# One-operation match in the expert routes, two pauses beside attention, and a layernorm applied by ScalarE alone

## The chip, the cores and the metric

The kernel runs on one core of a Trainium2 chip. The metric is the device time of one execution in microseconds (us). A core has TensorE (PE, with its weight load PEld), VectorE (DVE), ScalarE (ACT), GpSimd (POOL) and SyncE (SP), each with its own instruction queue; they run side by side and wait for each other by semaphores.

## The reference

The input is `x` of 8 batches, each 512 tokens of 128 numbers, in 32-bit floats. Six layers of different kinds are added to it one after the other:

```python
x = x + 0.5 * _L0_ffn_ref(_layernorm(x, axis=-1), L0_ffn_w_gate, L0_ffn_w_up, L0_ffn_w_down)
x = x + _L0_attn_ref(_layernorm(x, axis=-1), L0_attn_Wq, L0_attn_Wk, L0_attn_Wv, L0_attn_Wo, L0_attn_bo)
x = x + 0.5 * _L0_ffn_ref(_layernorm(x, axis=-1), L0_ffn_w_gate, L0_ffn_w_up, L0_ffn_w_down)
x = x + 0.5 * _L1_ffn_ref(_layernorm(x, axis=-1), L1_ffn_Wg, L1_ffn_W1, L1_ffn_W2, L1_ffn_W3)
x = x + _L1_attn_ref(_layernorm(x, axis=-1), L1_attn_w_qkv, L1_attn_w_out, L1_attn_b_out, L1_attn_gamma, L1_attn_beta)
x = x + 0.5 * _L1_ffn_ref(_layernorm(x, axis=-1), L1_ffn_Wg, L1_ffn_W1, L1_ffn_W2, L1_ffn_W3)
```

`_L0_ffn_ref` is a gated feed-forward whose inputs and weights are quantized to 4-bit floats in blocks of 16. `_L0_attn_ref` is softmax attention with 16 heads of 64 numbers. `_L1_ffn_ref` is a mixture of 8 experts with hidden size 256: every token goes to its two best experts, and their results are added with the softmax of the two scores as weights:

```python
top_v, top_i = jax.lax.top_k(gate_out, K)
probs = jax.nn.softmax(top_v, axis=-1)
...
    w_e = jnp.sum(probs * (top_i == e), axis=-1)
```

`_L1_attn_ref` is "efficient attention" of 6 layers: keys are normalized over the features and queries over the tokens, and `context = k^T v` (128x128) replaces the table of all pairs. The layernorm that the kernel calls `y` stands in front of its first layer: the residual stream inside `_L1_attn_ref` begins with a normalized `x`.

## The kernel before

A batch is held as `xs[b]`, 128 partitions by 4 chunks (`NC`) by 128. The first stage computes the feed-forward of all batches, interleaved with attention. Attention goes over 64 pairs of heads (`g`). The order of TensorE's and SP's work is written out by hand there: a list of steps (scores `pS`, projections `pq`, `pk`, `pv`, transposes `pT`, products `po`, output `py`) is run through once for each `g`. One kind of step, "ffn", calls `beside()`: it takes one step from a queue of other plans, that is, it issues that plan's instructions up to and with its next TensorE operation. `plan.pause()` puts an empty step into a plan, so that its next TensorE operation comes one "ffn" step later. The feed-forwards after attention of batches 0 to 6 and the first route stand in that queue, one behind the other; the feed-forward of batch 6 is the last.

After attention everything is ordered by a planner, `Plan.order`, before the kernel is built: each operation has an engine and an estimated time, and among those ready, the engine takes the one with the lowest key, the offset of its stage in the table `LATER` minus the longest path of estimates behind it. What comes out is one fixed order for each engine. Pauses are skipped there. The stages are: feed-forward of batch 7; phase 0 of the experts for batches 0 to 3 (A) and 4 to 7 (B); efficient attention over pairs of batches (k = 0, 2, 4, 6); phase 1 of the experts for A and B.

A stage of experts consists of a route, the gathering of tokens by expert, the expert products, and a combine. The route (`class Route`) scores the tokens (`gate`), picks the two best experts (`choose`, VectorE), counts tokens before each token with two products (`ranks`, L1035 and L1036), turns the counts into places in a table of slots (`bases`, `places`), and inverts this table: for each of 40 columns (`NR`) and 128 rows, which token sits there. The inversion goes over 8 parts (`tokens_part`), each for 4 chunks of tokens:

- `match` (L1125, VectorE): is the token's slot column equal to the column number? 128x160 into `in_slot`.
- `code` (L1140, GpSimd): `in_slot` times the number of the token, `code_no`, 128x160.
- `match_rows` (L1133, VectorE): is the token's row equal to the row number? 128x512 into `at_row`.
- `sums` (L1148, TensorE): four products of `at_row` and `in_slot` into one bank.
- `add` (L1156, L1158, VectorE): the bank into `acc`.

After the last part, `tables` (L1173 to L1179, VectorE) makes `tokens`, which the gathers read (L1215, an indirect DMA issued by GpSimd), and `targets` makes `places`, for the scatters (L1331). The buffers `in_slot` and `at_row` alternate between two, so that a match waits for the sums two parts before; in the first route, beside attention, there is one buffer of each. The route is computed four times: in the first route, B of phase 0, A and B of phase 1.

The expert stage has `g` (L1272 to L1277) and products at L1267 and L1315. The combine gathers the results token by token (L1384, GpSimd) and adds them to `x` (L1392, VectorE).

A layernorm (`class Norm`) takes its sums on VectorE (L390), and the reciprocal root in a chain of small GpSimd operations (`newton`, L369 to L374). It is applied by `on_vector` (L407, VectorE, one tensor_scalar for each chunk) or `on_scalar` (L415, ScalarE, one activation for each chunk). In `linear`, `begin` makes `y` from `x` with three chunks on VectorE and one on ScalarE; each of the 6 layers then applies its own layernorm with two chunks on each, and GpSimd adds a bias of 128x512 to `y` (L1466).

In the tail of attention L457, L468 and L469 are the quantizing of a feed-forward's hidden values on VectorE, L582 and L600 its last products; L708 is the row maximum `nmax`, L771 the division `oT`, which waits for `r`, the reciprocal row sums that go through a DMA (`wide`), L804 the output products.

## Time and profile before

| what | us |
|---|---|
| median of 3 timed runs | 2004.69 (2001.33 to 2011.76) |
| the profiled execution's own time | 1894.55 |
| its span | 1892.8 |
| TensorE, granted clock | 0.945 of full |
| GpSimd, busy | 962.0 |

The profile is of one execution. Its page splits the span into 40 equal slices (47.3 us each) and gives the busy tenths of every engine and the granted clock in tenths:

```profile
PE   3799999999999999999998998889659998798980
DVE  5475766775685776676657657557879998667543
ACT  2566666665665675666763654434457776353540
POOL 2345453443453453443443537676664444375786
PEclk8899999999999999999998999889979999698995
```

Slices 3 to 24 are the attention stage, 25 to 28 phase 0 of the experts, 29 to 35 efficient attention, and the rest phase 1. A digit 9 means 90% or more. The chain that ended last, by engine and by line:

```profile
PE 50%; DVE 23%; ACT 10%; POOL 9%; issue 4%; DMA 2%; SPq 0%; POOLq 0%; ACTq 0%; DVEq 0%
```

The share of an engine in the chain says how much of the span was spent waiting for it along one path; it is an average over stages with different limits.

### The profile page before, as it was taken

The numbers are of one execution on the slowest core, as the hardware profiler recorded it, in microseconds if no ns is written. First come the engines' busy times: TensorE is split into PE (matmuls) and PEld (weight loads), VectorE is DVE, ScalarE is ACT, GpSimd is POOL, SyncE is SP. The second block draws the span as 40 slices with busy tenths as digits, with TensorE's granted clock in tenths as the row PEclk, the third lists the DMA queues.
The fourth block names the chain that finished last, engine by engine and source line by source line (L and its number), as shares of the span: only waits on it lengthen the run. The fifth ranks groups of instructions, "written<-read, shape, count | busy, mean of one in ns | idle before, by whom it ended". The sixth has DMA issues, their size and how long they took to land.

```text
span 1892.8 us, 32338 instructions
## 1 busy us (share of the span) xinstructions
PE 1676.1 (89%) x10249; PEld 1132.1 (60%) x10249; DVE 1281.7 (68%) x3266; ACT 1073.6 (57%) x2842; POOL 962.0 (51%) x1643
## 2 busy tenths in 40 slices
PE   3799999999999999999998998889659998798980
PEld 2455656656556556556665566666548877676650
DVE  5475766775685776676657657557879998667543
ACT  2566666665665675666763654434457776353540
POOL 2345453443453453443443537676664444375786
PEclk8899999999999999999998999889979999698995
DMA  5477668567765776775683772215100000022314
GB/s 168 103 171 178 137 153 187 140 150 171 160 158 146 165 171 140 164 176 134 174 185 93 181 171 80 58 43 122 48 15 1 2 1 1 23 68 54 75 53 127
DMA packets 439253, 215.10 MB, mean 114 GB/s; under 512 B 349648, under 2 KB 392848, under 8 KB 439088
## 3 DMA queue, kind: packets, MB, share of 16 engines
q1 hardware_dynamic: 428608, 192.95, 42.7%
q0 software_dynamic: 9536, 19.55, 4.5%
q8 instruction: 86, 1.41, 0.3%
q14 instruction: 79, 0.65, 0.1%
q10 hardware_dynamic: 944, 0.54, 0.1%
HBM read 28.53 MB, written 100.53 MB: 68 GB/s over the span
## 4 chain that ended last, share of the span: by engine, by line
PE 50%; DVE 23%; ACT 10%; POOL 9%; issue 4%; DMA 2%; SPq 0%; POOLq 0%; ACTq 0%; DVEq 0%
PE po L763 9%; PE pS L699 9%; PE bank L1267 4%; ACT pe L711 4%; PE pT L749 3%; DVE nmax L708 3%; PE bank L600 2%; PE pv L685 2%; PE bank L541 2%; PE bank L1315 2%; PE pk L677 2%; PE bank L1148 2%; PE pq L671 2%; PE bank L424 2%; POOL work L1384 2%
## 5 line engine op out<-in xcount | busy, mean ns | idle before, releaser
L711 ACT ACTIVATE pe<-pS,nmax 128x512 f32<-128x512 f32 x512 | 348.4, 688 | 167.6 <-DVE nmax L708 135.8
L708 DVE TENSOR_REDUCE nmax<-pS 128x2 f32<-128x1024 f32 x256 | 310.6, 1214 | 75.7 <-PE pS L699 75.3
L720 POOL COPY pe_h<-pe 128x1024 uint16<-128x1024 uint16 x256 | 271.6, 1087 | 148.1 <-ACT pe L711 72.8
L699 PE MATMUL pS<-kT,qT 64*128 64x512 f32 x1024 | 291.9, 647 | 0.2
L763 PE MATMUL po<-aT,v 128*64 128x256 f32 x2048 | 239.2, 384 | 1.6 <-ACT kT L679 0.8
L787 POOL COPY wide<-rsum 128x512 uint16<-128x512 uint16 x128 | 76.4, 626 | 294.1 <-DVE rsum L783 294.1
L763 PEld LDWEIGHTS po<-aT,v 128*64 128x64 f32 x2048 | 142.9, 138 | 117.7 <-ACT pe L711 22.7
L1267 PE MATMUL bank<-wall,xgT 128*128 x320 | 156.8, 630 | 9.2 <-ACT xgT L1255 7.3
L749 PE MATMUL pT<-ident,pe 128*128 128x128 f32 x1024 | 137.3, 275 | 4.7 <-ACT pe L711 4.6
L749 PEld LDWEIGHTS pT<-ident,pe 128*128 128x128 f32 x1024 | 116.8, 141 | 23.1 <-ACT pe L711 17.8
L752 ACT COPY aT<-pT 128x512 f32<-128x512 f32 x192 | 107.5, 599 | 24.7 <-PE pT L749 23.0
L1272 ACT ACTIVATE g<-bank 128x256 f32<-128x256 f32 x160 | 61.0, 384 | 94.0 <-PE bank L1267 78.7
L699 PEld LDWEIGHTS pS<-kT,qT 64*128 64x128 f32 x1024 | 77.7, 186 | 57.8 <-issue 43.1
L1276 DVE SCALAR_TENSOR_TENSOR g<-g,bank 128x256 f32<-128x256 f32 x160 | 66.8, 417 | 64.9 <-ACT g L1272 64.5
L562 DVE SCALAR_TENSOR_TENSOR h<-h,bank 128x176 f32<-128x176 f32 x120 | 39.4, 329 | 100.7 <-ACT h L559 100.7
L541 PEld LDWEIGHTS bank<-wgu,xqT 128*128 128x128 f32 x480 | 76.2, 194 | 47.9 <-issue 20.4
L711 ACT ACTIVATION_READ_ACCUMULATOR pe<-pS,nmax 128x1 f32 x512 | 103.7, 202 | 0.0
L1267 PEld LDWEIGHTS bank<-wall,xgT 128*128 128x128 f32 x320 | 58.8, 199 | 73.5 <-issue 33.0
L541 PE MATMUL bank<-wgu,xqT 128*128 128x176 f32 x480 | 96.3, 327 | 6.3 <-ACT xqT L537 4.3
L771 DVE TENSOR_TENSOR oT<-po,r 128x256 f32<-128x256 f32 x128 | 52.0, 419 | 66.5 <-DMA r<-wide_d 34.5
L424 PE MATMUL bank<-ident,work 128*128 128x128 f32 x436 | 69.8, 289 | 28.1 <-DVE work L407 25.6
L685 PEld LDWEIGHTS pv<-wv_sb,hT 128*128 128x128 f32 x512 | 66.3, 193 | 43.5 <-ACT aT L752 21.7
(400 smaller groups left out, 3668.6 us busy)
## 6 DMA issues: line engine op xcount, KB each, us to landing
pe_d<-pe_h SPq DMA_DIRECT2D x256, 256.0 KB, 2.4
wide_d<-wide SPq DMA_DIRECT2D x64, 256.0 KB, 2.1
aT<-pe_d SPq DMA_TRANSPOSE x256, 3.8
xg<-work SPq DMA_DIRECT2D x12, 256.0 KB, 2.5
yg<-yo SPq DMA_DIRECT2D x10, 256.0 KB, 3.4
yt<-yo SPq DMA_DIRECT2D x10, 256.0 KB, 2.4
x<-in_x SPq DMA_DIRECT2D x8, 256.0 KB, 4.4
yk<-yg SPq DMA_DIRECT2D x8, 256.0 KB, 4.2
```

The lines of the kernel that those rows point to most:

```text
L424: nc.tensor.transpose(ps[:, c, :], src[:, c, :], ident)
L541: nc.tensor.matmul(ps[:, j * FH : (j + 1) * FH], m["xqT"][:, c * P : (c + 1) * P], wgu[:, j, cols], start=True, stop=True,)
L685: nc.tensor.matmul(ps[:, c, :], hT[:, c * P : (c + 1) * P], wv_sb[:, cols(g)], start=True, stop=True,)
L699: nc.tensor.matmul(ps[:, j, :], qTs[g][rows, c * P : (c + 1) * P], kTs[g][rows, :], start=True, stop=True,)
L708: nc.vector.tensor_reduce(nmax, ps, AX.X, ALU.max, negate=True)
L711: nc.scalar.activation(pe[:, j, :], ps[:, j, :], AF.Exp, bias=nmax[:, j : j + 1], accum_out=sums[g][:, 2 * c + j : 2 * c + j + 1],)
L720: nc.gpsimd.tensor_copy(split, pe[:, j, :].bitcast(U16).rearrange("p (n h) -> p h n", h=2))
L749: nc.tensor.transpose(ps[:, k, :], pe[:, j, k * P : (k + 1) * P], ident)
L752: nc.scalar.copy(dst, ps)
L763: nc.tensor.matmul(po[rows, :], vs[g][:, k, rows], aT[:, :, j, k, :], start=(k == 0), stop=(k == NC - 1),)
L787: nc.gpsimd.tensor_copy(split[:, h, :].rearrange("p (n d) -> p n d", d=DH), src[:, h, :, None].to_broadcast([P, NC * 2, DH]),)
L1267: nc.tensor.matmul(ps, xT[:, s, :], wall[:, bass.ds(at[s], 2 * HID)], start=True, stop=True)
```

## The change

The change has four parts. In each part of a route `match` becomes four tensor_scalar operations on VectorE (128x40 each, one for each chunk), which compare and multiply with the token's number in one operation; `code` on GpSimd is gone. Three pauses are put between `choose` and `ranks`, and two in front of the eight parts; they act in the route beside attention. `begin` applies the layernorm `y` with four activations on ScalarE. The planner's table `LATER` has other offsets, and the estimate of a match is 4 x 130 ns.

```diff
 LATER = {
-    ("combine", 0, 0): -5000,
-    ("combine", 0, 1): 6600,
-    ("combine", 1, 0): -15100,
-    ("combine", 1, 1): 199700,
-    ("experts", 0, 0): 3300,
-    ("experts", 1, 0): 90500,
-    ("experts", 1, 1): -37300,
-    ("ffn",): 11300,
-    ("linear", 0): 10800,
-    ("linear", 2): 6800,
-    ("linear", 4): -300,
-    ("linear", 6): 4600,
-    ("route", 0, 0): -10000,
-    ("route", 0, 1): -27200,
-    ("route", 1, 0): -6400,
-    ("route", 1, 1): 76900,
+    ("combine", 0, 1): 10915,
+    ("combine", 1, 0): 27994,
+    ("combine", 1, 1): -28254,
+    ("experts", 0, 0): 3252,
+    ("experts", 1, 0): 90518,
+    ("experts", 1, 1): -127932,
+    ("ffn",): -188793,
+    ("linear", 0): 10802,
+    ("linear", 2): 6768,
+    ("linear", 6): 4568,
+    ("route", 1, 0): -3116,
+    ("route", 1, 1): 76948,
 }
...
             ch = plan.add("DVE", 12 * 290 + 600, choose, taken)
+            for _ in range(3):
+                plan.pause()
             rk = plan.add("PE", product(n * E, 2), ranks, [ch], bank=True)
...
                 def match(_):
-                    bc = [P, NC, NR]
-                    ins = r["in", k] = mem(f"in_slot{k % 2}", bc)
-                    nc.vector.tensor_tensor(
-                        ins, r["slot"][:, j, cs, None].to_broadcast(bc),
-                        numbers[:, None, :NR].to_broadcast(bc), ALU.is_equal,
-                    )
+                    ins = r["in", k] = mem(f"in_slot{k % 2}", [P, NC, NR])
+                    for i in range(NC):
+                        c = q * NC + i
+                        nc.vector.tensor_scalar(
+                            ins[:, i, :], numbers[:, :NR], r["slot"][:, j, c : c + 1],
+                            code_no[:, j * NN + c : j * NN + c + 1], ALU.is_equal, ALU.mult,
+                        )
...
-                def code(_):
-                    bc = [P, NC, NR]
-                    nc.gpsimd.tensor_tensor(
-                        r["in", k], r["in", k],
-                        code_no[:, j * NN + q * NC : j * NN + (q + 1) * NC, None].to_broadcast(bc),
-                        ALU.mult,
-                    )
-
...
-                w = plan.add("DVE", dve(NC * NR), match, [pl, *users[-2:-1]])
-                w = plan.add("POOL", pool(NC * NR), code, [w])
+                w = plan.add("DVE", 4 * 130, match, [pl, *users[-2:-1]])
...
+            for _ in range(2):
+                plan.pause()
             for k in range(2 * MG):
                 tokens_part(k)
...
             def part(i, b):
-                op = plan.add("DVE", 3 * 343, lambda _: ln.on_vector(ys[b], xs[b], i, [0, 1, 2]), [ln.op])
-                op2 = plan.add("ACT", 390, lambda _: ln.on_scalar(ys[b], xs[b], i, [3]), [ln.op])
-                return [op, op2]
+                return plan.add(
+                    "ACT", 4 * 290 + 100, lambda _: ln.on_scalar(ys[b], xs[b], i, range(NC)), [ln.op]
+                )
```

Over four routes of eight parts this takes away 32 VectorE operations of 128x160 and 32 of GpSimd, and adds 128 VectorE operations of 128x40; in `begin` 24 operations go from VectorE to ScalarE.

## The prediction

> **What bounds the kernel now.** I read the table of busy shares first, then stretches of the span one by one, because the kernel is a row of stages with different limits; then, in each stage that the change touches, the waits of the engine that sets its pace. First the busy share, then the windows (stretch, length, busy PE, PEld, DVE, ACT, POOL with counts, TensorE clock, DMA share, GB/s):
>
> ```profile
> PE 1676.1 (89%) x10249; PEld 1132.1 (60%) x10249; DVE 1281.7 (68%) x3266; ACT 1073.6 (57%) x2842; POOL 962.0 (51%) x1643
> 1000.00:1050.00 50.00, 41.07 (x259) 27.42 (x258) 37.29 (x107) 18.35 (x46) 19.64 (x32) 0.86 0.40 102
> 1200.00:1300.00 100.00, 89.33 (x414) 62.56 (x414) 57.34 (x186) 37.19 (x82) 70.20 (x95) 0.85 0.28 73
> 1395.00:1472.16 77.16, 69.14 (x491) 58.23 (x492) 72.20 (x238) 53.66 (x183) 41.12 (x121) 0.98 0.01 1
> 1472.16:1515.68 43.52, 41.45 (x303) 35.14 (x303) 40.22 (x133) 32.82 (x121) 20.59 (x60) 1.00 0.00 1
> 1740.00:1893.00 153.00, 99.56 (x554) 69.32 (x552) 66.80 (x186) 54.92 (x120) 115.74 (x149) 0.84 0.35 86
> ```
>
> Attention (to 1138.7) is TensorE's: full, except in 1000 to 1050, where the first route runs beside it and TensorE loses 9 us. Phase 0 of the mixture of experts (1139 to 1339) is TensorE's with holes. In the linear-attention stage TensorE and VectorE are both above 92% of a 43.5 us layer. After 1740 GpSimd decides; see the last part of the change.
>
> **The route beside attention.** TensorE's timeline (start, length, line, operation, idle before and who ended it), then the tile `in_slot` with its waits:
>
> ```profile
> 1020.86 1.93 PE L1148 MATMUL bank<-in_slot,at_row 128*128 128x40 f32 x8 [8.27 <-POOL in_slot L1140]
> 1022.72 2.08 PE L699 MATMUL pS<-kT,qT 64*128 64x512 f32 x4
> 1024.72 5.57 PE L763 MATMUL po<-aT,v 128*64 128x256 f32 x32
> L1125 DVE TENSOR_TENSOR in_slot<-slot,numbers x8: 314/316/772, 1019.6 to 1052.2; 128x160 f32<-128x160 f32 x8
> L1140 POOL TENSOR_TENSOR in_slot<-in_slot,code_no x8: 766/768/886, 1020.0 to 1052.7; 128x160 f32<-128x160 f32 x8
>   POOL in_slot L1140: 20.3, 8
> ```
>
> TensorE stands 8.27 us until the first code operation ends. What follows is slow too: these three groups take 1.93, 2.08 and 5.57, where the same forms take 1.08, 1.13 and 3.67 from 1030 on, so 3.7 more. Two later parts make it wait 0.66 each. Together 8.3 + 3.7 + 1.3 = 13.3 us. The Trainium skill (TensorE: Matmul & The Clock Gate, Part 1) says that the array falls to half clock after an idle stretch of about 3.4 us and needs about as long of work to leave it. This bears on the new stall below.
>
> In the changed program's order the pauses put the ranks products a step later, with 11.7 us of TensorE work (four pS, po, pq, pk, pv, pT by their rows) between them and the first sums. VectorE needs 11.5 to 12.4 us from ranks to the first match. I take a wait of 1 us, too short to cool the clock: gain 12.3. If the cover fails, the wait is at most the old one.
>
> The price of a part: 4 tensor_scalar of 128x40 in place of one 128x160. No row has this form. A lone 128x40 tensor_scalar takes 0.18, and small VectorE operations start 0.11 to 0.22 after each other; four are 0.45 at the least, 0.8 at the most, I take 0.6 for four, against the 0.25 between starts of L1125 and L1133 now: +0.35. The skill speaks against the split: VectorE: DVE Perf Modes (The TRN2 errata) has a fixed 58 cycles per instruction at 0.96 GHz from SBUF, paid per tile, hence (58+160)/0.96 = 227 ns against 4 x (58+40)/0.96 = 408, +0.18. Over 32 parts that is +5.8 by the rule and +11.2 by my rows; I take the rows, since 316 was measured where the rule has 227. It matters only in the routes after attention, where a part's chain sets the pace. Against it stand 32 GpSimd operations of 0.77 to 0.83 (25.6 us) and two handovers a part. A second rule speaks against it: Advanced Engine Details and Errata (VectorE Performance Modes) says that two-port VectorE operations and GpSimd block each other. The trace agrees:
>
> ```profile
> 1659.43 0.83 DVE L1173 TENSOR_SCALAR tok_A<-acc_A 128x40 f32<-128x40 f32 x1
> 1658.95 1.27 POOL L1466 TENSOR_TENSOR y<-y,bout_sb 128x512 f32<-128x512 f32 x1 [0.23 <-DVE acc_A L1158]
> ```
>
> The 0.18 us form lasts until GpSimd's bias ends (1660.22). GpSimd computes in about 27% of 1000 to 1050 without the code operations; some 0.2 us a part, hidden by attention's TensorE work once sums stand one to a step. By the rule all 8 parts could wait up to 1 us; even that is under the roughly 3 us between parts.
>
> **The end of attention gives part back.** The five pauses push the last feed-forward's (ffn 6) products back five steps. Now the L600 product stands between the last pS and the last pT and covers the softmax:
>
> ```profile
> 1120.72 0.76 DVE L771 TENSOR_TENSOR oT<-po,r 128x256 f32<-128x256 f32 x2 [3.35 <-DMA r<-wide_d]
> 1121.39 1.21 DVE L708 TENSOR_REDUCE nmax<-pS 128x2 f32<-128x1024 f32 x1
> 1121.25 2.94 PE L600 MATMUL bank<-wdn,hqT 128*128 128x128 f32 x24
> ```
>
> In the changed order the last nmax stands behind L457, L468 and L469 of ffn 6 (0.81 each between starts = 2.4), which stand behind or between the two oT, and L468 waits 1.0 for ScalarE's h_mg: nmax 3.4 later, exp, pT, rsum and the r round trip with it (7.1 from rsum to oT). On the old times TensorE would stand from 1121.3 to about 1126.8 and still have L600 to do, which then fills the wait for r: the end moves by 5.5 or so. By the rule above such a stop also cools the clock (up to +3); by the row alone it doesn't. I take +6; ends 0 (the wait for r falls away) and +9. **Attention: -12.3 + 6 = -6.3**, ends -12 and 0. The early gathers (1058 to 1070, used at 1139) move some us and have room.
>
> **Phase 0, route B** (1222 to 1245). A part's chain is match, handover, 0.83 code, handover, sums; codes start 1.7 apart, with expert gathers queued between them on GpSimd. Without them a part is 0.83 + 0.15 - 0.35 = 0.6 shorter; six parts in a row give 4. TensorE does expert work meanwhile, but waits for those gathers (0.8 to 0.9, three times) and for g (2.98). **-4**, ends -10 and +5, since the planner's changed keys permute the order here most: route (0,1) goes from -27200 to 0, so later, and ffn 7 from 11300 to -188793, so ahead of the experts; TensorE's instructions are the same 7211 either way, so only waits can change, and the row of nearest size is the three waits above, 2.5 together.
>
> **Combine and linear attention.** GpSimd's gathers for combine B (1.25 each) stand in front of the first layer's rstd:
>
> ```profile
> 1386.57 2.14 PE L424 MATMUL bank<-ident,work 128*128 128x128 f32 x8 [24.70 <-DVE work L407]
> 1403.98 6.45 DVE L407 TENSOR_SCALAR y<-x,y_m,y_g 128x128 f32<-128x128 f32 x6
> 1404.18 6.16 POOL L1466 TENSOR_TENSOR y<-y,bout_sb 128x512 f32<-128x512 f32 x5
> ```
>
> The layernorm's six y operations (1.6 by their usual start distance) take 6.45 because they block with five biases: 4.8 lost. With the change ScalarE does all 24 of VectorE's: +24 x 0.41 = 9.9 us for an engine 71% busy, -24 x 0.26 = -6.2 for the one at 92%. A pair starts 0.9 later (4 activations, 1.66, in a row). In the new GpSimd order the first layer's rstd stands some three gathers earlier (-3.7) while the last combine ends 2 to 3 later. -4.8 - 3.7 + 0.9 + 2.5 = **-5**; ends -15 (more of the 24.7 closes) and +5.
>
> **Phase 1.** Route A (1637 to 1661): TensorE waits 8.29 and 2.73; codes sit between biases. Parts run in pairs of 2.6 us of VectorE: **-3** (-6 to +2). Route B (1715 to 1740): match pairs already wait for sums, and expert operations between them fill the time: **0** (-3 to +3).
>
> **The end.** From here GpSimd never idles:
>
> ```profile
> 1740.41 0.94 POOL L1215 DMA_INDIRECT y<-xg,tokens_B  x1 [3.17 <-DVE tokens_B L1179]
> 1883.98 0.94 POOL L1384 DMA_INDIRECT work<-yt,rows_A  x1 [0.30 <-issue]
> ```
>
> 39 gathers, 39 scatters, 32 combine gathers, the same number after: the end shifts with tokens_B, and everything above counts only through it. SP's and DMA's counts do not change.
>
> **Sum.** -6.3 - 4 - 5 - 3 = -18.3. The profiled execution took 1894.55 (span 1892.8), so about 1876 for it. The timed median, 2004.69, lies 110 above; nothing in the trace explains that, so I carry the difference in us: **1986**.
>
> **Rivals.** (a) *The gain is returned*: 0.25. The tail of attention goes cold (+9 instead of +6), route B of phase 0 gives nothing since TensorE is 89% busy there, and combine and route A give 1 each: -3.3 - 0 - 1 - 1 = about -5, 1999. For it: three of four gains lie under other work. Against it: the 13.4 us are TensorE's own. (b) *Slower*: the re-planned linear stage. The chain has the layers:
>
> ```profile
> 1472.16 1.47 DVE work L407 x2
> 1515.68 1.53 DVE work L407 x2
> ```
>
> 3.3 us of 43.5 are free on VectorE. Biases block L407 by about 1 us each, three times a layer now. If the new order lets all eight meet one, a layer takes 48.5, six layers +30: -18 + 30 = +12, 2017. It decides from 3 us a layer. Against it: the order stays near cyclic and counts are the same. 0.15. (c) *More*: the 24.7 us wait closes by ten more and route stalls vanish: -32, 1973. 0.15. (d) *It does nothing where it counts*: tokens_B does not move, as experts alone set it; contained in (a). Forecast: 0.45.
>
> A difference under 0.5% (10 us) can't be told from none. The forecast's own range is 1977 to 1996. Faster: 0.9 x 0.45 + 0.15 = 0.56; slower: 0.15 x 0.8 + some of (a)'s bad end (0.10) = 0.22; same 0.22. The range 1965 to 2018 leaves out the ends of (b) and (c).
>
> **What would show it.** The wait at L1148 near 1020 under 2 us, and no slow po behind it; a wait of about 5 before the last pT; attention ending near 1132; y in ScalarE rows; layer starts still 43.5 apart; tokens_B about 18 earlier. It is wrong if layers grow by over 1 us or tokens_B stays at 1740.

## The result, and the profile after

The changed kernel took 2019.51 us (median of 4 runs, 2017.90 to 2024.04) beside 2003.01 for the kernel before (median of 4, 2000.27 to 2011.76). The ratio is 1.0093, with a 95% interval of 1.0066 to 1.0120. The forecast was 1986, so it had the wrong sign.

The later runs went to four chips, and the chip matters more than the change. The unchanged kernel took 2012 to 2013 us on two of them (called "late chips" below, for a reason that the last section shows) and 1893 to 1896 on the two others ("prompt chips"). The profile shown of before, with a span of 1892.8, is like the second kind, while its timed median is like the first. Every ratio below is therefore taken against the unchanged kernel run beside it on the same chip, and traces are compared within one kind of chip.

The page of the changed kernel, from a late chip; the busy share of each engine, and the chain that ended last:

```profile
PE 1708.2 (85%) x10249; PEld 1152.2 (57%) x10249; DVE 1288.8 (64%) x3338; ACT 1079.6 (54%) x2866; POOL 934.5 (46%) x1611
...
PE 49%; DVE 22%; ACT 9%; POOL 7%; another core or an unknown queue 5%; issue 5%; DMA 2%; POOLq 0%; ACTq 0%; DVEq 0%
```

The counts are what the change makes of them (VectorE 72 more, ScalarE 24 more, GpSimd 32 fewer). But the span is 2016.7, and 5% of the chain, about 100 us, waits for something that the profile can't name. The chain of before has no such entry. One might blame the change, but the unchanged kernel, profiled on a late chip, has it too (4% of a span of 2015.2). So the comparison by stages has to be made on a prompt chip. There the same changed program (run c1_after) has a span of 1896.9 and a chain without that entry. Stage by stage, from the same instructions in both traces (`mT` is the divided `context`, which VectorE makes once for each linear layer and pair of batches):

| stretch | before | after (c1_after) | difference | forecast |
|---|---|---|---|---|
| start to the last `py` product | 1138.7 | 1145.9 | +7.2 | -6.3 |
| to `tokens_B`, phase 0 | 106.2 | 107.6 | +1.4 | -4 |
| to the first gather of combine B | 98.4 | 94.6 | -3.8 | -5, with the next two |
| to the first `mT` | 7.8 | 8.1 | +0.3 | |
| first to last `mT` (the six layers, four pairs) | 321.7 | 321.4 | -0.3 | |
| to `tokens_B`, phase 1 | 67.3 | 67.3 | 0.0 | -3 |
| to the end | 152.7 | 152.0 | -0.7 | 0 |
| span | 1892.8 | 1896.9 | +4.1 | -18.3 |

Each column is one execution. Two executions of one other kernel on prompt chips (e4_later and e7_later, below) differ by up to 2 us in the first five stretches and by 8 in the one up to `tokens_B` of phase 1 (63.0 and 71.0). So of the differences here only attention's is clear by itself: in the nine kept traces whose attention is that of before it ends at 1136.1 to 1138.7, in the four with the whole change's attention at 1144.1 to 1145.9.

Attention is where the forecast failed most, by 13.5 us of 22.4. Its windows after, in the columns of the windows shown of before (stretch, length, busy PE, PEld, DVE, ACT, POOL, clock, DMA share, GB/s); the first lies 15 us later than its counterpart of before, since the route comes later:

```profile
1015.00:1065.00 50.00, 44.20 (x238) 26.81 (x234) 39.21 (x103) 23.31 (x58) 14.11 (x18) 0.83 0.55 139
1065.00:1120.00 55.00, 54.02 (x336) 31.82 (x336) 40.87 (x74) 35.42 (x91) 29.74 (x33) 1.00 0.71 171
1120.00:1146.00 26.00, 20.34 (x148) 16.57 (x144) 6.95 (x13) 5.05 (x10) 3.11 (x4) 0.87 0.35 85
```

TensorE is busier in the route (44.2 of 50 beside 41.07), but at a lower clock, 0.83 beside 0.86, and with fewer products (238 beside 259): the busier stretch does not do more work. And the last 26 us of attention now have a hole of 5.7 us and a clock of 0.87. They were nearly full before:

```profile
1112.00:1139.00 27.00, 25.80 (x193) 18.64 (x192) 8.00 (x15) 9.76 (x25) 6.40 (x8) 1.00 0.66 142
```

### The route: TensorE's wait went, and two others and a cold clock came

TensorE's timeline on the prompt chip, from the ranks products to the first parts:

```profile
1019.46 0.39 PE L1032 MATMUL bank<-both,ones 128*128 128x128 f32 x2
...
1023.79 1.97 PE L745 MATMUL pT<-ident,pe 128*128 128x128 f32 x8 [1.82 <-ACT pe L707]
1025.69 1.87 PE L695 MATMUL pS<-kT,qT 64*128 64x512 f32 x4
...
1036.50 1.08 PE L1139 MATMUL bank<-in_slot,at_row 128*128 128x40 f32 x8 [1.27 <-DVE at_row L1132]
1038.50 1.97 PE L745 MATMUL pT<-ident,pe 128*128 128x128 f32 x8 [0.92 <-ACT pe L707]
1041.06 1.90 PE L1139 MATMUL bank<-in_slot,at_row 128*128 128x40 f32 x8 [0.59 <-DVE at_row L1132]
1042.89 2.08 PE L695 MATMUL pS<-kT,qT 64*128 64x512 f32 x4
```

The 8.27 us wait before the first sums is now 1.27, close to the 1 us forecast. But the waits of this stretch, with one more of 1.05 at 1063.23, still sum to 5.65 (9.59 before), because two transposes `pT` now wait for the softmax. And the groups at half speed (those that take up to twice their usual time) are more, not fewer. Against their full-speed forms (1.05 for pT, 1.13 for pS, 1.12 for pq, 1.0 for sums), the slow groups between 1023 and 1052 took 7.5 us longer, where before lost 3.7.

Why the softmax is late is seen in VectorE's timeline of the same execution:

```profile
1019.53 0.42 DVE L767 TENSOR_TENSOR oT<-po,r 128x256 f32<-128x256 f32 x1
1020.37 0.69 DVE L464 SCALAR_TENSOR_TENSOR xh<-x_mg,xh 128x512 f32<-128x512 f32 x1 [0.42 <-ACT x_mg L460]
1021.09 0.69 DVE L465 SCALAR_TENSOR_TENSOR xh<-x_mg,xh 128x512 f32<-128x512 f32 x1
1021.70 1.22 DVE L704 TENSOR_REDUCE nmax<-pS 128x2 f32<-128x1024 f32 x1
1022.84 0.68 DVE L750 COPY aT<-pT 128x512 f32<-128x512 f32 x1
1023.43 0.28 DVE L1038 COPY base<-bank 128x128 f32<-128x128 f32 x1
...
1034.91 0.93 DVE L1124 TENSOR_SCALAR in_slot<-numbers,slot,code_no 128x40 f32<-128x40 f32 x4
```

The counts (`bank`, ready at 1019.85) are first read at 1023.43. Before, the copy into `base` started 0.4 us after the ranks products (1009.11 after 1008.71). In the step to which the pauses move the ranks, VectorE has a feed-forward's quantizing, an `oT`, `nmax` and `aT` ahead of it, with a wait of 0.42 for ScalarE: 3.6 us. From the end of ranks to the end of the first `at_row` VectorE now takes 16.6 us, where the trace of before had 11.8. Of the 4.8 more, 3.2 lie in front of `base` and 1.6 behind it, where a second `nmax` and the longer match come in between. The same queue delays `nmax`, and with it `pe` and `pT`.

That the first wait still came out near 1 us is luck. VectorE's way from the first ranks product to the first match grew to 15.7 us, and TensorE's cover grew with it only because TensorE itself waited 1.82 for pT and lost 1.7 at half speed behind it. In the trace from the late chip, where the groups behind that pT run at full speed, the first sums wait 2.52.

### The end of attention

TensorE's timeline, the same execution:

```profile
1126.97 1.97 PE L745 MATMUL pT<-ident,pe 128*128 128x128 f32 x8 [5.34 <-ACT pe L707]
...
1129.73 5.29 PE L759 MATMUL po<-aT,v 128*64 128x256 f32 x32
```

This is the forecast's stall, in its place and almost in its size: 5.34 us before the last pT (5.5 forecast), and a cold clock behind it (po takes 5.29 instead of 3.67, pT 1.97 instead of 1.07). VectorE shows the forecast's cause too: the last `nmax` stands behind the quantizing of the feed-forward, and starts at 1124.83, 3.4 later than before (1121.39).

```profile
1123.10 0.89 DVE L464 SCALAR_TENSOR_TENSOR h<-h_mg,h 128x704 f32<-128x704 f32 x1 [0.52 <-ACT h_mg L460]
1124.02 0.89 DVE L465 SCALAR_TENSOR_TENSOR h<-h_mg,h 128x704 f32<-128x704 f32 x1
1124.83 1.22 DVE L704 TENSOR_REDUCE nmax<-pS 128x2 f32<-128x1024 f32 x1
```

The Trainium skill (TensorE: Matmul & The Clock Gate, Part 1) has the array cold after about 3.4 us of idle, and this place agrees.

The two 1.97 of the route do not fit that rule as simply: 1.82 us of idle, or 1.27 and 0.92 with a product between them, were enough. The page does say that the window runs freely, so that the point of change moves with its phase. In these traces too the same wait is followed by slow groups in one execution and not in another: after the same 1.82 on the late chip pT takes 1.32 and the next pS runs at full speed, and no slow group follows the 1.05 at 1063.23 here, while slow groups follow both waits of 1.05 in a1_no_pauses, below. So the measured rows decide here and not the rule.

### The profile page after: what moved, and what is told of

Same layout as the page of the kernel before. It is cut to its first block, busy times and chain, and to the rows that moved or that the text cites. A ratio compares the mean times of both kernels' runs of the same rounds, so it can differ in the third digit from the quotient of the medians.

```text
span 2016.7 us, 32388 instructions
## 1 busy us (share of the span) xinstructions
PE 1708.2 (85%) x10249; PEld 1152.2 (57%) x10249; DVE 1288.8 (64%) x3338; ACT 1079.6 (54%) x2866; POOL 934.5 (46%) x1611
## 4 chain that ended last, share of the span: by engine, by line
PE 49%; DVE 22%; ACT 9%; POOL 7%; another core or an unknown queue 5%; issue 5%; DMA 2%; POOLq 0%; ACTq 0%; DVEq 0%
PE po L759 8%; PE pS L695 8%; PE bank L1259 4%; ACT pe L707 4%; DVE nmax L704 3%; PE pT L745 3%; PE bank L1307 3%; PE bank L596 2%; PE pv L681 2%; PE bank L420 2%; PE bank L537 2%; PE bank L1139 2%; PE pk L673 2%; PE pq L667 2%
## 5 line engine op out<-in xcount | busy, mean ns | idle before, releaser
L745 PE MATMUL pT<-ident,pe 128*128 128x128 f32 x1024 | 139.7, 278 | 11.5 <-ACT pe L707 11.1
L1307 PE MATMUL bank<-wall,gT 128*128 x640 | 92.7, 303 | 24.5 <-ACT gT L1292 12.2
L1307 PEld LDWEIGHTS bank<-wall,gT 128*128 128x128 f32 x640 | 88.0, 217 | 34.9 <-issue 19.4
L1512 ACT ACTIVATE work<-bank,nmk 128x128 f32<-128x128 f32 x192 | 68.1, 376 | 55.8 <-DVE nmk L1504 55.8
```

The source lines that it names most:

```text
L745: nc.tensor.transpose(ps[:, k, :], pe[:, j, k * P : (k + 1) * P], ident)
L1307: nc.tensor.matmul(ps[:, s * D : (s + 1) * D], gT[:, s, k, :], wall[:, bass.ds(at[s] + (2 * HID + k * D), D)], start=(k == 0), stop=(k == ...
L1512: nc.scalar.activation(c4(ek)[:, c, :], pk.tile[:, c * D : (c + 1) * D], AF.Exp, bias=nmk[:, i, c : c + 1], accum_out=sk[:, i, c : c + 1],)
```

## The experiments

### The change's parts one by one, on a late chip

The unchanged kernel took 2011.9 us. Run c0_before is that kernel once more, without an edit.

> The kernel before, unchanged, with a new profile. The profile shown of it has a span of 1892.8 us, 110 under the median of its timed runs, and no stretch in which TensorE, VectorE and ScalarE all stand while GpSimd issues gathers, except 11.5 us at 1846.8; the profile of the changed kernel has 17 such holes of over 1.5 us, 85 us in all, and a span of 2016.7. Theory A (such holes are in most executions of both kernels, and the first profile lacked them): a span of about 2000 with 70 to 110 us of holes beside rows of gathers. Theory B (the holes come with the change): a span near 1893 and no holes beyond those shown.

Measured: 0.9994 (0.9971 to 1.0017). Its profile has a span of 2015.2, with holes as theory A says; the last section counts them.

The five pauses alone:

```diff
             ch = plan.add("DVE", 12 * 290 + 600, choose, taken)
+            for _ in range(3):
+                plan.pause()
...
+            for _ in range(2):
+                plan.pause()
             for k in range(2 * MG):
```

> Only the five pauses are added; match, code, layernorm and the planner's offsets stay. Theory 'attention is the loss' (the tail of attention waits 5.5 us more, and the route gains less than that): +2 to +5 us against before. Theory 'attention gains' (the prediction's step): -6. Theory 'the loss is in the planned part' : within 3 us of before, as the planner's order is not touched.

Measured: 1.0037 (1.0014 to 1.0060), that is +7. In its trace attention ends at 1144.7, where c0_before has 1137.2.

The match alone, with `code` removed:

```diff
-                    nc.vector.tensor_tensor(
-                        ins, r["slot"][:, j, cs, None].to_broadcast(bc),
...
+                        nc.vector.tensor_scalar(
+                            ins[:, i, :], numbers[:, :NR], r["slot"][:, j, c : c + 1],
...
-                w = plan.add("POOL", pool(NC * NR), code, [w])
```

> Only match and code become four tensor_scalar on VectorE (and the planner's estimates with them); no pauses, layernorm and offsets of before. Four of them took 0.93 us in the changed kernel where I had 0.6. Theory 'the split costs': +5 to +10 us. Theory 'the handover to GpSimd was the cost': -5 to -10 us, of which about 3 in the route beside attention. Theory 'the order decides': any value, with the planned part's stage ends moved by more than the 32 operations explain.

Measured: 1.0097 (1.0055 to 1.0139; 5 runs). Attention ends at 1142.3, 5 us later than in c0_before, out of some 20 in all; where the rest arises stays open. TensorE's first wait is no shorter, 8.55; nearly the same row is shown with a1_no_pauses below.

The y layernorm on ScalarE alone:

```diff
-                op = plan.add("DVE", 3 * 343, lambda _: ln.on_vector(ys[b], xs[b], i, [0, 1, 2]), [ln.op])
-                op2 = plan.add("ACT", 390, lambda _: ln.on_scalar(ys[b], xs[b], i, [3]), [ln.op])
-                return [op, op2]
+                return plan.add(
+                    "ACT", 4 * 290 + 100, lambda _: ln.on_scalar(ys[b], xs[b], i, range(NC)), [ln.op]
+                )
```

> Only the layernorm y goes to ScalarE alone; everything else as before. Theory of the prediction: -3 to -5 us, since six y operations that took 6.45 us on VectorE no longer block with GpSimd's biases. Rival: 0 to +5 us, because each pair of batches starts 0.9 us later and ScalarE is 71% busy there.

Measured: 0.9986 (0.9965 to 1.0008), no difference that this can tell.

What follows: both parts that touch attention make it longer, each alone. The rest of the time on this chip is disturbed by the long waits of the last section, in all four kernels.

### The whole change and its table, on a prompt chip

The unchanged kernel took 1895.46 us. The whole change, without an edit:

> The changed kernel again, beside its parts on one chip. Attention ended 6.9 us later in its profile than in the new profile of the kernel before (1144.1 against 1137.2), and what follows took 872.6 against 878.0 in single profiles. Theory 'the loss is attention': +5 to +9 us. Theory 'the planned part loses too' (the +16.5 of the first comparison): +14 to +20.

Measured: 1896.42, ratio 1.0007 (0.9995 to 1.0018). On this chip the change is worth nothing either way. Both theories had expected a loss, and attention does end 7.2 later, so the stages after it give most of that back.

The planner's table alone (the first hunk of the change's diff):

```diff
 LATER = {
...
-    ("ffn",): 11300,
...
-    ("route", 0, 1): -27200,
...
+    ("ffn",): -188793,
...
 }
```

> Only the planner's offsets are those of the changed kernel. Attention should end as before (1137). Theory 'the offsets fit the changed operations and not the old ones': +5 to +25 us, all of it after attention. Theory 'the offsets are the gain': -5 to -20. Theory 'offsets only permute': within 3 us.

Measured: 1888.65, ratio 0.9964 (0.9953 to 0.9974), that is -6.8.

All of the change but the table:

```diff
 LATER = {
...
-    ("ffn",): -188793,
...
+    ("ffn",): 11300,
...
+    ("route", 0, 1): -27200,
...
 }
```

> All of the change but the offsets, which are those of before. Match alone with the old offsets took 903.7 us after attention in its profile, against 878.0 for before and 872.6 for the changed kernel. Theory 'the new offsets repair the order that the new operations upset': 15 to 25 us slower than the changed kernel, +30 or so against before. Theory 'match costs by its own work': within 5 us of the changed kernel.

Measured: 1900.44, ratio 1.0031 (1.0018 to 1.0044). With the table, c1_after has 1.0007: beside the other three parts the table gives 4.6, within the 5 us of the second theory and far from the 15 to 25 of the first.

A GpSimd memset of 128x1 in front of each gather of the kernel before (each scatter has one already, L1330), which opens their dense rows:

```diff
+    rest = const.tile([P, 1], F32, name="rest")
...
+        nc.gpsimd.memset(rest, 0.0)
         nc.gpsimd.indirect_dma_start(
             x[:, s, :], None, xg[:, :],
...
+                    nc.gpsimd.memset(rest, 0.0)
```

> The kernel before, with a small memset on GpSimd in front of each gather (scatters have one already). In the profiles, engines stand for 4 to 22 us until a signal of TensorE is seen, mostly beside rows of gathers issued back to back. Theory 'unbroken rows of gathers hold back the signals': a memset breaks them, the holes shrink from 70 to 90 us to under 30, and the time falls by 40 us or more. Theory 'any indirect DMA does it': no change, within 5 us, as a memset of 0.11 fits into the pause of 0.30 between gathers. Theory 'GpSimd is just the bound': +5 to +10.

Measured: 1.0003 (0.9993 to 1.0013). It was meant for the late chips, and this chip has none of their holes, so it says only that the memsets cost nothing that can be seen.

### The change without one part, on the same prompt chip

The unchanged kernel took 1895.92 us. Each of the first three kernels is the whole change with one part undone; the diffs are those of the single parts above, reversed. Without the pauses:

```diff
-            for _ in range(3):
-                plan.pause()
...
-            for _ in range(2):
-                plan.pause()
```

> The changed kernel without its pauses. In the changed kernel attention ended 7.2 us later than in the kernel before (1145.9 against 1138.7), with a wait of 5.34 before a late pT. Theory 'the pauses push the last feed-forward out of its cover': the end of attention comes back by 2 to 4 us, as match alone still loses 4 to 5 there (1142.3 on another chip, against 1137.2): about 2 us faster than the changed kernel. Theory 'the pauses pay in the route': 3 to 8 us slower than it.

Measured: 0.9974 (0.9966 to 0.9983). Beside c1_after the pauses cost 0.33%, 6.3 us. TensorE's timeline of this kernel, the sums that wait and what follows two of them:

```profile
1020.69 1.93 PE L1137 MATMUL bank<-in_slot,at_row 128*128 128x40 f32 x8 [8.57 <-DVE at_row L1130]
...
1033.83 1.18 PE L1137 MATMUL bank<-in_slot,at_row 128*128 128x40 f32 x8 [1.05 <-DVE at_row L1130]
1034.94 2.08 PE L695 MATMUL pS<-kT,qT 64*128 64x512 f32 x4
1036.95 1.65 PE L667 MATMUL pq<-hT,wq_sb 128*128 128x512 f32 x2
...
1052.82 1.06 PE L1137 MATMUL bank<-in_slot,at_row 128*128 128x40 f32 x8 [1.05 <-DVE at_row L1130]
...
1054.87 1.89 PE L667 MATMUL pq<-hT,wq_sb 128*128 128x512 f32 x2
1056.55 1.77 PE L1137 MATMUL bank<-in_slot,at_row 128*128 128x40 f32 x8
1058.12 1.95 PE L745 MATMUL pT<-ident,pe 128*128 128x128 f32 x8
1059.99 2.07 PE L695 MATMUL pS<-kT,qT 64*128 64x512 f32 x4
```

Without the handover to GpSimd the waits are longer: 8.57 where before had 8.27, and twice 1.05 where before had 0.66. The releaser has changed from `in_slot` to `at_row`. In the trace of before, `at_row`, which the sums need too, ended at 1020.49, and the code operation at 1020.81:

```profile
1019.81 0.68 DVE L1133 TENSOR_TENSOR at_row<-rf,numbers 128x512 f32<-128x512 f32 x1
1019.98 0.83 POOL L1140 TENSOR_TENSOR in_slot<-in_slot,code_no 128x160 f32<-128x160 f32 x1 [1.00 <-DVE in_slot L1125]
```

So removing the code could save 0.3 at most, while the new match puts `at_row` 0.85 after its start instead of 0.23, 0.6 later. What is left is 0.3 more, the difference measured.

Attention ends at 1143.0 here, 4.3 later than before, and these waits alone are 1.1 of it. The rest is speed: behind the two waits of 1.05, groups at half speed took 1.5 and 3.4 us longer than their usual forms. (This is more than the 4.3; other places of attention give some back.) Behind the waits of 0.66 in the trace of before there is none:

```profile
1033.93 1.09 PE L1148 MATMUL bank<-in_slot,at_row 128*128 128x40 f32 x8 [0.66 <-POOL in_slot L1140]
1034.94 1.13 PE L699 MATMUL pS<-kT,qT 64*128 64x512 f32 x4
```

In the two kernels on late chips that have the match and no pauses (e2_match, b2_match_later), slow groups follow one of the two waits of 1.05 each.

Without the match:

```diff
-                w = plan.add("DVE", 4 * 130, match, [pl, *users[-2:-1]])
+                w = plan.add("DVE", dve(NC * NR), match, [pl, *users[-2:-1]])
+                w = plan.add("POOL", pool(NC * NR), code, [w])
```

> The changed kernel with match and code as before (GpSimd multiplies again). Theory 'the four operations (0.93 us where one of 0.25 between starts was) eat what the code saved': within 3 us of the changed kernel, with attention ending 1 us earlier or at the same time. Theory 'the code's 25 us on GpSimd matter after attention': 5 to 10 us slower than it. The offsets are those of the changed kernel.

Measured: 1902.27, ratio 1.0032 (1.0005 to 1.0059; 7 runs). That is 0.25% or 4.7 us above c1_after, but the two intervals together leave room for 0.5% and for nothing: whether the match gives anything beside the other three parts is not shown. The profiles of the two executions, with spans of 1895.3 and 1896.9, show no gain. Attention ends at 1142.1 here.

Without the layernorm on ScalarE (y on VectorE and ScalarE again):

```diff
-                return plan.add(
-                    "ACT", 4 * 290 + 100, lambda _: ln.on_scalar(ys[b], xs[b], i, range(NC)), [ln.op]
-                )
+                op = plan.add("DVE", 3 * 343, lambda _: ln.on_vector(ys[b], xs[b], i, [0, 1, 2]), [ln.op])
+                op2 = plan.add("ACT", 390, lambda _: ln.on_scalar(ys[b], xs[b], i, [3]), [ln.op])
+                return [op, op2]
```

> The changed kernel with the layernorm y split over VectorE and ScalarE as before. Theory 'y on ScalarE gives 3 to 5 us': 3 to 5 us slower than the changed kernel. Theory 'it gives nothing' (alone it gave 0.9986 of before on another chip, with an interval from 0.9965 to 1.0008): within 2 us of it.

Measured: 0.9981 (0.9971 to 0.9992): beside c1_after, ScalarE's y costs 0.26%, 4.9 us, the opposite of the first theory. The stages have it in the linear layers: from the first mT to the last it takes 313.9 us without ScalarE's y and 321.4 with it. Of these 7.5 us, 6.1 are made up for earlier (from tokens_B to the first gather of combine B it takes 100.7 without it and 94.6 with it). TensorE's longest wait near the start of these layers, in c1_after and then in this kernel, where before had 24.70:

```profile
1388.62 1.29 PE L420 MATMUL bank<-ident,work 128*128 128x128 f32 x4 [20.12 <-DVE work L403]
```

```profile
1384.08 2.01 PE L420 MATMUL bank<-ident,work 128*128 128x128 f32 x8 [11.22 <-DVE work L403]
```

With y left on VectorE the wait is less than half of that before. With ScalarE it is nearly the old one, and 3.30 more are lost at 1411.36. The two kernels with the table and without match and pauses show the same pair: 11.22 with y on VectorE (e4_later) and 20.21 with y on ScalarE (e6_begin_later, next). So the gain that the forecast gave to ScalarE's y belongs to the other order of operations, and ScalarE's y takes more than half of it back. Which operation of the new order makes the difference was not traced.

ScalarE's y and the new table, without match and pauses:

```diff
 LATER = {
...
-    ("ffn",): 11300,
...
+    ("ffn",): -188793,
...
 }
...
+                return plan.add(
+                    "ACT", 4 * 290 + 100, lambda _: ln.on_scalar(ys[b], xs[b], i, range(NC)), [ln.op]
+                )
```

> Only the layernorm on ScalarE and the new offsets; no pauses, match and code as before. The offsets alone gave 0.9964 (1888.7 against 1895.5). Theory 'parts add up': 1886, faster than both kernels, since attention ends as before and the planned part has the gain. Theory 'the offsets were fitted to the layernorm in VectorE': 1890 or more.

Measured: 1891.49, ratio 0.9985 (0.9972 to 0.9998), 0.21% (4 us) above the table alone, as the second theory has it. The same sign and size as in a3_no_begin, from the other side.

### Can the pauses be had without their price? On a late chip

The unchanged kernel took 2012.93 us. The whole change, with the last feed-forward stepped five steps further ahead, so that TensorE's order at the end of attention is again as it was before:

```diff
-                if len(queue) > 1 and queue[0][1] > AHEAD and queue[1][1] < AHEAD:
+                if len(queue) > 1 and queue[0][1] > AHEAD and queue[1][1] < AHEAD + queue[1][3]:
...
+                queue.append([ffn(b), 0, -1, 5 if b == NB - 2 else 0])
```

> The changed kernel, with the last feed-forward beside attention (ffn 6) stepped five steps further ahead while the route runs, so that the order of TensorE's work at the end of attention is that of the kernel before (L596, the last product, again in front of the last pT). The five pauses stay. Theory 'the loss of the pauses is the lost cover at the end': attention ends 6 us or more earlier than in the changed kernel (1145.9), and the time falls by as much, to 0.997 of before. Theory 'VectorE is the limit while the route runs, and what is put beside it delays it': attention ends within 2 us of 1145.9.

Measured: 1.0050 (1.0028 to 1.0072). The tail is mended: no wait over 0.34 us is left around the last po. But attention ends at 1146.5. The waits stand in the route instead (1.08 for x_mg, 1.71 and 2.04 before sums, for VectorE's `at_row`, 1.12 for pT), with 3.23 at 1093.12. So the theory that the loss is the tail alone falls. The feed-forward work has to be done somewhere, and beside the route it makes VectorE late.

The new offsets, and the new match only in the routes after attention:

```diff
-                w = plan.add("DVE", dve(NC * NR), match, [pl, *users[-2:-1]])
-                w = plan.add("POOL", pool(NC * NR), code, [w])
+                if name == "r0":
+                    w = plan.add("DVE", dve(NC * NR), match, [pl, *users[-2:-1]])
+                    w = plan.add("POOL", pool(NC * NR), code, [w])
+                else:
+                    w = plan.add("DVE", 4 * 130, match_code, [pl, *users[-2:-1]])
```

> The new offsets, and the four tensor_scalar only in the three routes after attention; the route beside attention has match and code as before. No pauses, layernorm as before. Theory 'match pays after attention and costs beside it': attention ends at 1137 to 1138.7 and the time is 4 to 6 us under that of the offsets alone (0.9964), 0.994 of before. Theory 'match gives nothing there': 0.9955 to 0.997.

Measured: 1.0029 (1.0011 to 1.0046), slower than both theories. Attention ends at 1137.5, as in the unchanged kernel. The table's gain was measured on prompt chips, and none of the kernels with the table shows it on a late one.

The new offsets and the new match everywhere (the table's hunk and the diff of e2_match):

```diff
 LATER = {
...
-    ("ffn",): 11300,
...
+    ("ffn",): -188793,
...
 }
...
+                w = plan.add("DVE", 4 * 130, match, [pl, *users[-2:-1]])
```

> The new offsets, and the four tensor_scalar in all four routes. Theory 'match costs about 5 us beside attention': 4 to 6 us slower than the kernel that has them only after attention, with attention ending near 1143. Theory 'the later end of attention is absorbed afterwards': within 2 us of it.

Measured: 1.0015 (0.9995 to 1.0036), attention to 1142.3. It is no slower than b1_match_planned, although its attention ends 4.8 us later. So on a late chip a later end of attention need not show in the time.

The kernel of b1_match_planned with the pauses and the feed-forward stepped ahead:

```diff
+            for _ in range(3):
+                plan.pause()
...
+            for _ in range(2):
+                plan.pause()
...
+                queue.append([ffn(b), 0, -1, 5 if b == NB - 2 else 0])
```

> The new offsets, the four tensor_scalar only after attention, the five pauses, and ffn 6 stepped five further ahead. Theory 'the pauses pay once the end keeps its cover': attention ends 3 to 5 us earlier than before (1134 to 1136), and the time is as much under that of the kernel without pauses: 0.991 to 0.993 of before. Rival: the extra feed-forward work beside the route delays VectorE's chain and the sums wait longer; attention ends at 1138 or later.

Measured: 1.0031 (1.0015 to 1.0047), attention to 1138.5. With the old match the pauses can be placed so that attention ends only 1 us later, within the spread of the unchanged kernel, but they still gain nothing.

### The best kernel again, and the dense rows again, on another prompt chip

The unchanged kernel took 1893.3 us. The table alone once more:

```diff
 LATER = {
...
-    ("ffn",): 11300,
...
+    ("ffn",): -188793,
...
 }
```

> The kernel before with the planner's new offsets alone, once more. Beside an unchanged kernel of 1895 us it measured 0.9964 (interval 0.9953 to 0.9974). If the offsets are worth those 6.8 us wherever they run: ratio 0.995 to 0.9975, also where the unchanged kernel takes 2000 to 2013. If their gain is lost where TensorE's signals come late (the combinations with these offsets measured 1.0015 to 1.0031 there): 0.999 to 1.003 on such a chip.

Measured: 1885.02, ratio 0.9954 (0.9938 to 0.9971; 6 runs). The gain is there on a second chip, -8.3 us. This kernel beats both, on prompt chips. It was not run on a late one.

The memsets in front of the gathers, unchanged from s1_spaced:

```diff
+        nc.gpsimd.memset(rest, 0.0)
         nc.gpsimd.indirect_dma_start(
```

> The kernel before with one GpSimd memset of 128x1 in front of each gather and scatter. Theory: where the unchanged kernel takes 2000 to 2013, TensorE's signals come late because of rows of indirect DMAs issued one right after another; the memset opens the rows, and the ratio falls to 0.95 to 0.985. Rival: the late signals have nothing to do with the density of the issues: 0.997 to 1.003. If the unchanged kernel takes 1895 in this call the row theory is not tested, and 1.000 is expected (measured before there: 1.0003).

Measured: 1.0009 (0.9995 to 1.0022). By its own terms this did not test the theory of dense rows, since the chip was prompt.

## Why the prediction was wrong

The step that failed is attention: -6.3 forecast, +7.2 measured, made of a gain of 12.3 that did not come and a loss of 6 that did. The gains of phase 0 and of phase 1 did not show either. What the first comparison lost beyond attention stays open (see the rivals).

**Attention, the gain of 12.3: this step failed.** The wait of 8.27 did become 1.27. But the step took VectorE's 11.5 to 12.4 us from ranks to the first match out of the trace of before, and put them behind the moved ranks unchanged. In the new place they took 15.7, with 3.6 us of attention's own work ahead of them. From the rows of c1_after: first wait -7.0; waits of later parts +0.3 (0.59 and 1.05 for 1.32); new waits of pT +2.7 (1.82 and 0.92); groups at half speed 7.5 for 3.7, +3.8. This leaves -0.2 of the 12.3. That the clock would stay warm after 1 us was the second mistake in the same step.

**The match beside attention, put at nothing: wrong as well.** The forecast let the price of a part matter only after attention, since TensorE's work would hide it. The match without the pauses ends attention at 1142.3 to 1143.0 in three kernels. In a1_no_pauses the waits of 0.66 became 1.05, and half speed behind them cost 4.9.

**The price of a part, 0.6 for four: mis-sized.** The tile of c1_after, minimum, median and maximum in ns:

```profile
L1124 DVE TENSOR_SCALAR in_slot<-numbers,slot,code_no x32: 292/299/1071, 1034.9 to 1069.4; 128x40 f32<-128x40 f32 x32
```

One takes 0.30 and the next starts 0.21 later, so four take 0.93: outside both ends, 0.45 and 0.8, and over twice the 0.41 by the rule that the forecast weighed. (The formula of the Trainium skill, VectorE: DVE Perf Modes, The TRN2 errata, divides the elements by a factor of the mode, which the forecast left at one; a larger factor would lie further off.) The row of before that the forecast took for nearest, 0.18, multiplies by fixed numbers; this form reads two columns of scalars, one value for each partition. Before had a row with two such columns, the layernorm:

```profile
L407 DVE TENSOR_SCALAR work<-y,l_m,l_g x96: 304/342/1380, 1333.5 to 1657.5; 128x128 f32<-128x128 f32 x96
```

With fixed numbers the operation takes 0.178 for 128x40 (L1173) and 0.199 for 128x70 (L454) in the same trace. An estimate from these two, stretched to 128x128, is 0.24. So L407's 0.342 has about 0.1 for its two columns, as the 0.30 has here. The maximum of 1071 is one of eight operations that ran 0.6 to 1.1 us beside a GpSimd copy and ended with it, as the forecast allowed.

**The tail, +6: right** in place and cause, and near in size: 5.34 of wait, 0.9 on pT and 1.6 on po make 7.8, within the ends of 0 and 9. Attention's change was to be the difference of these two terms. With 0.2 in place of 12.3 it is a loss of 7.6, and 7.2 is what the ends of attention show. The undone parts show that pauses and match each cost and do not add up. Attention ends at 1136.1 to 1138.7 with neither, at 1142.3 to 1143.0 with the match alone, at 1142.1 and 1144.7 with the pauses alone, and at 1144.1 to 1145.9 with both.

**Phase 0, route B, -4: wrong, +1.4.** The chain of a part was taken as match, code, sums, and the 0.98 of code and handover as its saving. But sums also wait for `at_row`. In this route's trace of before it ended 0.3 before the code in four of the eight parts, and after it in the four others; the first part's rows in a1_no_pauses show a part 0.3 longer, not 0.6 shorter. Other kernels on the prompt chips do not shorten the stretch either: 107.4 with the new match and the old table (e5_old_later), 107.1 to 107.8 with the old match and the new table, 106.2 before. In c1_after the sums of this route go from 1230.58 to 1252.24, where before had 1226.19 to 1242.02: more products of the experts now stand between them.

**Combine and linear attention, -5: -3.8 measured, for another reason.** It was mostly laid to ScalarE's y. Undoing that makes the kernel 4.9 us faster, and the offsets alone give -6.8 to -8.3. That the sum was near is luck, two errors of opposite sign.

**Route A and B of phase 1, -3 and 0:** together 0.0 to tokens_B. Route A's sums, first start to last end, went from 18.3 to 17.6; TensorE's first wait there is 7.80 for 8.29. With executions of one program 8 us apart in this stretch, neither forecast can be judged.

**The end, 0: right.** After tokens_B every kernel on the prompt chips takes 152 to 155 us, whatever came earlier. So tokens_B of phase 1 is a good place to read a change, within the spread of single executions: 1740.1 before, 1744.9 after, 1730.3 and 1737.7 with the table alone.

**The rivals.** The slower one (layers of 48.5 us) did not happen: the four pairs of batches took 321.4, before 321.7. (a), the gain given back, is nearest to what the prompt chips show. In the first comparison the loss was 16.5 us. Attention ends 7 later there (1144.1, beside 1137.2 in c0_before), but by b2_match_later it is not sure that all of this reaches the total on a late chip. The spans of these two executions are only 1.5 us apart, while single executions of the unchanged kernel spread over more than 20. Where the rest, 9 us or more, comes from stays open.

**Carrying the 110 us** between profile and median over in full was a guess about the unknown, and was stated as one. The last section shows what it stood for.

## What to carry to other kernels

When an operation is moved to another step of a hand-written order, read the queue of every engine at the new place: the distance between two operations belongs to the place, not to the operations. When a handover is removed from a join of two inputs, the gain is bounded by the other input's end, here 0.3 us of the 0.98 removed. And count short stalls of TensorE at more than their length: the waits of 1 to 2 us in c1_after's route were followed by 7.5 us of lost speed, one of 8.27 by 3.7.

## What the runs showed of the hardware

One program, two times: 1893 to 1896 us on two chips, 2012 to 2013 on two others, with every execution on a chip within about 1% of the median there. In the traces of the late chips engines stand idle for long after the work that they seem to wait for has ended. VectorE's timeline of the changed kernel on a late chip, phase 1:

```profile
1767.98 0.19 DVE L1006 COPY G_B<-bank 128x32 f32<-128x32 f32 x1 [20.78 <-remote]
1779.89 0.39 DVE L1006 COPY G_B<-bank 128x32 f32<-128x32 f32 x3 [11.73 <-remote]
```

and TensorE's, which makes those banks:

```profile
1752.96 1.95 PE L998 MATMUL bank<-wg_sb,work 128*128 128x8 f32 x16
1768.32 3.55 PE L998 MATMUL bank<-wg_sb,work 128*128 128x8 f32 x16 [13.40 <-issue]
```

The products ended at 1754.9, and VectorE went on at 1767.98. The profile knows no releaser for this wait ("remote"), so that VectorE waited for a late signal of TensorE is a reading, not something shown. The unchanged kernel does the same, in its own trace from a late chip:

```profile
1773.55 0.19 DVE L1010 COPY G_B<-bank 128x32 f32<-128x32 f32 x1 [22.67 <-remote]
```

TensorE's products had ended at 1759.6 there. Stretches of over 1.5 us in which TensorE, VectorE and ScalarE all stand, from 1130 to the last operation of these three: 3 with 16.2 us in before on a prompt chip, 5 with 19.6 in c1_after, but 23 with 75.5 in c0_before and 15 with 74.4 in the changed kernel on late chips. Most lie beside GpSimd's rows of gathers and scatters. What makes the chips late was not settled. The memsets that were to test the rows' density ran on prompt chips both times. What the runs do show is that it isn't the change, and that late and prompt chips lie some 120 us apart, more than any edit tried here moved the time.
